# An LSTM step in two halves of its units: two gate banks, one product instruction, a state turned by halves

## The chip, the cores and the metric

The kernel runs on one core of a Trainium2 chip. The metric is the device time of one execution, in microseconds (us). Times shown are medians of several executions; the profile is of one more execution, and its own time stands beside its span, the time from its first to its last recorded instruction. PE is TensorE (PEld its weight loads), DVE is VectorE, ACT is ScalarE, POOL is GpSimd, SP is the engine that issues most DMAs.

## The reference

The input is x, 32 batches of 512 nodes by 256 features, in fp32, with an adjacency of integers. Two layers follow, each a graph attention and a feed-forward part, each on a layer norm of x and added to it:

```python
x = x + gnn0(layernorm(x), adj)      # typed attention, 4 heads
x = x + ffn0(layernorm(x))           # a Mamba-2 block
x = x + gnn1(layernorm(x), adj)      # one-head attention
x = x + ffn1(layernorm(x))           # an LSTM, with sums over its outputs
```

The last part is the one that matters here. It is an LSTM with 256 units over the 512 nodes as time:

```python
gates = xp + h @ W_hh.T                        # xp = x @ W_ih.T + b_ih + b_hh
i, f, g, o = split(gates, 4)
c = sigmoid(f) * c + sigmoid(i) * tanh(g)
h = sigmoid(o) * tanh(c)
```

Of its outputs, two logits for each step decide whether h enters a running sum; the result is 2 h plus the sum before the step times `fw_att` plus the sum after it times `bw_att`.

## The kernel before

Two phases follow each other. The first goes through the 32 batches one by one and does everything up to the LSTM (`layers_per_batch`); it leaves x in DRAM as X3, by time. It also reorders the LSTM's weights on POOL, between other work (`recurrence_weights`, with its helper `ordered`), into a DRAM tile. The second phase is `recurrence`: 512 steps for all 32 batches at once. There the program orders PE, DVE and ACT by hand: these engines run the instructions in the order of the code (`tc.manual_schedule`).

**Layout of a step.** The 256 units are four quarters (Q = 4) of 64 (J = 64). A quarter's results lie in 32 partitions (GB = 32, the batches), so that a [128, 64] tile holds all units of all batches. Sigmoids are computed as tanh of half the argument; the factors of one half are put into the weights, so that a step has tanh alone. `z` is a tile of 5 × 64 columns: the cell, then the four gates in the order forget, input, candidate, output.

**PE in a step.** `h_part` (L1260) adds the state's product with W_hh to the gates: for each part of the columns, each half k of the state (DK = 2) and each quarter q one matmul with 32 stationary columns, so that four of them stand side by side in the array. The parts are the forget gate (64 columns), input and candidate (128), output and the two logits (66), each in a PSUM bank of its own (tiles pg0, pg1, pg2). Then `x_part` (L1250) starts the next step's banks with its part of x: it turns the finished products of x (`xu`) through an identity. Then PE makes one eighth of the x products of a later group of 8 steps (`units`, L1236, two matmuls), and in 4 of 16 steps it first turns a normalised tile of x (L1174). A matmul of fp32 is two instructions in the profile.

**ACT and DVE in a step.** ACT takes one tanh for each part (L1320), later the tanh of the cell (L1330), then the copies out of PSUM (L1179, L1237). DVE makes two products in the tile `ab` (L1322 forget times cell, L1323 input times candidate), the new cell (L1328), the state hh (L1333) and its transpose by blocks of 32x32 into h (L1335), which is what PE's next h part waits for. Behind it come the masked state g (L1342, it reads the logits), the running sum pp (L1345), and one piece of extra work (`extra`: statistics and norms of later x, or a piece of the output of the 16 steps before, L1160 to L1213).

Buffers: z, ab, tc and h have three each (pool `st`); pg0 has one bank, pg1 and pg2 two each, pxt one and pu two, which fills the eight banks. In profile lines below, q and u of L630 are small tiles of the first phase.

Of the kernel before, what the change touches and what calls it, by code (L numbers as in the profile page):

```python
# [9 lines left out]
F32 = mybir.dt.float32  # L10
# [3 lines left out]
AF = mybir.ActivationFunctionType  # L14
ALU = mybir.AluOpType
# [4 lines left out]
P = 128  # L20
# [3 lines left out]
DK = D // P  # L24
# [9 lines left out]
GB = 32  # L34
# [995 lines left out]
def recurrence_weights(nc, pool, a, wr):  # L1030

    Q, J = 4, 64
    W = 4 * J + 2
    nx, nh = DK * Q * 4 * J, DK * Q * W
    n0 = nx + nh  # L1040
    half = (0.5, 0.5, 0.5, 1.0)
    for_x, for_h = (0, 3, 1, 2), (1, 0, 3, 2)

    def tile_(p, n, tag):
        return pool.tile([p, n], F32, tag=tag, name=tag)

    def ordered(raw, n, order, s):
        t = tile_(P, W, "rwt")
        nc.gpsimd.memset(t[:n, 4 * J :], 0.0)
        for to, g in enumerate(order):  # L1050
            nc.gpsimd.tensor_scalar(t[:n, to * J : (to + 1) * J], raw[:n, g * J : (g + 1) * J], half[g] * s, None, ALU.mult)
        return t


    wl = tile_(P, 2 * DK, "rwl")
    for q in range(Q):
        for l in range(2):
            nc.sync.dma_start(
                out=wl[q * 32 : (q + 1) * 32, l * DK : (l + 1) * DK],
                in_=a.wl[q : q + 1, l * J : (l + 1) * J].rearrange("o (k p) -> p (o k)", p=32),  # L1060
            )
    yield
    nc.gpsimd.tensor_tensor(wl[:, :DK], wl[:, DK:], wl[:, :DK], ALU.subtract)
    bl = tile_(P, 2, "rbl")
    nc.sync.dma_start(out=bl, in_=a.bl.to_broadcast([P, 2]))
    b = [tile_(P, 4 * J, f"rwraw{n}") for n in range(2)]
    for t, src in zip(b, (a.bih, a.bhh)):
        nc.sync.dma_start(out=t[:Q], in_=src.rearrange("o (q r) -> (o q) r", q=Q))
    yield
    nc.gpsimd.tensor_tensor(bl[:, 0:1], bl[:, 0:1], bl[:, 1:2], ALU.subtract)  # L1070
    nc.gpsimd.tensor_tensor(b[0][:Q], b[0][:Q], b[1][:Q], ALU.add)
    t = ordered(b[0], Q, for_x, 1.0)
    yield
    nc.sync.dma_start(out=wr[0][:, n0 + 2 * J + 8 : n0 + 2 * J + 9], in_=bl[:, 0:1])
    nc.sync.dma_start(out=wr[1].rearrange("o (q w) -> (o q) w", q=Q), in_=t[:Q, : 4 * J])
    yield
    nc.sync.dma_start(out=wr[0][:, n0 + 2 * J : n0 + 2 * J + 8], in_=wr[1].rearrange("o (u p) -> p (o u)", p=P))
    yield
    for n, src in enumerate((a.fw, a.bw)):
        t = tile_(P, W, "rwt")  # L1080
        for q in range(Q):
            nc.sync.dma_start(out=t[q * GB : (q + 1) * GB, :J], in_=src[q : q + 1, :].to_broadcast([GB, J]))
        yield
        nc.gpsimd.tensor_scalar(t[:, :J], t[:, :J], 0.5, None, ALU.mult)
        yield
        nc.sync.dma_start(out=wr[0][:, n0 + n * J : n0 + (n + 1) * J], in_=t[:, :J])
        yield
    for n, (src, s) in enumerate(((a.wih, 1.0), (a.whh, 0.5))):
        for k in range(DK):
            for q in range(Q):  # L1090
                raw = tile_(P, 4 * J, f"rwraw{q % 2}")
                cols = slice(q * 4 * J, (q + 1) * 4 * J)
                if n == 0:
                    nc.sync.dma_start(out=raw, in_=src[k * P : (k + 1) * P, cols])
                else:
                    for r in range(Q):
                        r0 = r * J + k * 32
                        nc.sync.dma_start(out=raw[r * 32 : (r + 1) * 32], in_=src[r0 : r0 + 32, cols])
                yield
                t = ordered(raw, P, (for_x, for_h)[n], s)  # L1100
                if n == 1:
                    nc.gpsimd.tensor_scalar(t[:, 4 * J : 4 * J + 1], wl[:, k : k + 1], 0.5, None, ALU.mult)
                yield
                w = (4 * J, W)[n]
                o0 = n * nx + (k * Q + q) * w
                nc.sync.dma_start(out=wr[0][:, o0 : o0 + w], in_=t[:, :w])
                yield


def recurrence(ctx, tc, c, a, X3, wr, out):  # L1110
# [3 lines left out]
    nc = tc.nc  # L1114
    T = X3.shape[0]
    Q, J = 4, 64
    W = 4 * J + 2
    G = CH // 2
    wp = ctx.enter_context(tc.tile_pool(name="rw", bufs=1))
    xp_ = ctx.enter_context(tc.tile_pool(name="rx", bufs=2))  # L1120
    st = ctx.enter_context(tc.tile_pool(name="rs", bufs=3))
# [115 lines left out]
        return lambda: nc.scalar.activation(xu[:, u, :], pu, AF.Identity, bias=bcol[:, u : u + 1])  # L1237


    PARTS = ((0, J), (J, 3 * J), (3 * J, W))  # L1240

    def x_part(t, xu):

        pg = [
            psg.tile([P, e - s], F32, tag=f"pg{n}", bufs=(1, 2, 2)[n], name=f"pg{n}_{t}") for n, (s, e) in enumerate(PARTS)
        ]
        r = (t % G) * GB
        for p, half, (s, e) in zip(pg, (1, 0, 1), ((0, J), (0, P), (J, P + 2))):
            for q in range(Q):
                nc.tensor.matmul(  # L1250
                    p[q * GB : (q + 1) * GB, :], xu[:, 2 * q + half, r : r + GB], turner[:, s:e],
                    start=True, stop=(t == 0),
                )
        return pg

    def h_part(pg, h, parts=PARTS, start=False):
        for p, (s, e) in zip(pg, parts):
            for k in range(DK):
                for q in range(Q):
                    nc.tensor.matmul(  # L1260
                        p[q * GB : (q + 1) * GB, :], h[:, k, :], whh[:, k, q, s:e],
                        start=(start and k == 0), stop=(k == DK - 1),
                    )

    with tc.manual_schedule(engines={mybir.EngineType.PE, mybir.EngineType.DVE, mybir.EngineType.Activation}):
        nxt = [None] * 2
# [7 lines left out]
        xu = {}  # L1274
# [2 lines left out]
        units(G, nxt[1], xu, 0)()  # L1277
        extra, turning = [], {}
        pg = x_part(0, xu[0])
        z = st.tile([P, 5 * J], F32, tag="z", name="z0")  # L1280
        nc.vector.memset(z[:, :J], 0.0)
        pp = ch.tile([P, CH + 1, J], F32, tag="pp", name="pp0")
        nc.vector.memset(pp[:, 0, :], 0.0)
        h = hh = None
        for t in range(T + 1):
# [14 lines left out]
                turning = {(5, 6, 10, 11)[n]: f for n, f in enumerate(turns)}  # L1300
            if last:

                pg = [psg.tile([P, W - 3 * J], F32, tag="pg2", name="pglast")]
                h_part(pg, h, PARTS[2:], True)
            elif t:
                h_part(pg, h)
            pgs = pg
            if not last:
                if t + 1 < T:
                    pg = x_part(t + 1, xu[(t + 1) // G * G])  # L1310

                g, u = divmod(t + 1, G)
                g = (g + 1) * G
                turned = [turning.pop(s)()] if s in turning else []
                if g < T:
                    turned.append(units(g, (xT if g < t0 + CH else nxt)[g // G % 2], xu, u))

                for (s0, e0), p in zip(PARTS, pgs):
                    e0 = min(e0, 4 * J)
                    nc.scalar.activation(z[:, J + s0 : J + e0], p[:, : e0 - s0], AF.Tanh)  # L1320
                ab = st.tile([P, 2 * J], F32, tag="ab", name=f"ab{t}")
                nc.vector.scalar_tensor_tensor(ab[:, :J], z[:, J : 2 * J], 1.0, z[:, :J], ALU.add, ALU.mult)  # L1322
                nc.vector.scalar_tensor_tensor(  # L1323
                    ab[:, J:], z[:, 2 * J : 3 * J], 1.0, z[:, 3 * J : 4 * J], ALU.add, ALU.mult
                )
                z2 = st.tile([P, 5 * J], F32, tag="z", name=f"z{t + 1}")
                cell = z2[:, :J]
                nc.vector.scalar_tensor_tensor(cell, ab[:, :J], 0.5, ab[:, J:], ALU.mult, ALU.add)  # L1328
                tc_ = st.tile([P, J], F32, tag="tc", name=f"tc{t}")
                nc.scalar.activation(tc_, cell, AF.Tanh, scale=0.5)  # L1330
                for f in turned:
                    f()
                nc.vector.scalar_tensor_tensor(hh[:, s, :], z[:, 4 * J :], 1.0, tc_, ALU.add, ALU.mult)  # L1333
                h = st.tile([P, DK, GB], F32, tag="h", name=f"h{t}")
                nc.vector.transpose(h.rearrange("p k b -> p (k b)"), hh[:, s, :])  # L1335
                z = z2
            if t:

                i = (t - 1) % CH
                p_, h_ = (pp_was, hh_was) if s == 0 and not last else (pp, hh)  # L1340
                g_ = st.tile([P, J], F32, tag="g", name=f"g{t}")
                nc.vector.scalar_tensor_tensor(  # L1342
                    g_, pgs[-1][:, J : J + 1].to_broadcast([P, J]), level, h_[:, i, :], ALU.is_gt, ALU.mult,
                )
                nc.vector.tensor_tensor(p_[:, i + 1, :], p_[:, i, :], g_, ALU.add)  # L1345
                if s == 0 and not last:
                    nc.vector.tensor_copy(pp[:, 0, :], p_[:, CH, :])
            if extra:
                extra.pop(0)()
        assert not extra and not turning  # L1350
        tot = wp.tile([P, J], F32, name="tot")
        nc.vector.tensor_tensor(tot, pp[:, CH, :], bw, ALU.mult)
# [112 lines left out]
```

## Time and profile before

| what | value |
|---|---|
| median of 3 executions | 4829.85 us (4828.24 to 4832.57) |
| the profiled execution, its time | 4838.21 us |
| its span | 4836.4 us |
| PE busy in the span | 4191.4 us (87%) |
| DVE busy | 3279.3 us (68%) |
| ACT busy | 3068.7 us (63%) |
| PE instructions | 52926 |
| granted TensorE clock, mean over the span | 0.965 |
| recurrence, first to last step | 3398 to 4768 us |

Busy PE is not PE at its peak, since matmuls overlap and their ends are modelled. A line of the timeline has a start in us from the span's start, a length, an engine, a line of the kernel, an operation, the tiles it writes and reads, the shapes and a count; several instructions in a row are merged into one line. A line of the groups has busy us and the mean ns of one, then the idle time ahead and what ended it. A line about one source line has the least, median and greatest duration in ns, and the first and last start in us. In the chain of waits, "issue" is time in which nothing that the profile shows was waited for, and ACTq is ACT's sequencer.

### The profile page before, as it was taken

How to read it: one execution, taken by the hardware profiler on the slowest of the kernel's cores; microseconds unless marked ns; L12 is line 12 of the kernel's file. 1: busy time of each engine (PE TensorE's matmuls, PEld its weight loads, DVE VectorE, ACT ScalarE, POOL GpSimd, SP SyncE). 2: the span in 40 equal slices, each digit the busy share in tenths (PEclk: the TensorE clock that was granted, in tenths of full speed). 3: DMA queues.
4: the chain of work that ended last, by engine and by line, in shares of the span. 5: the costliest groups of instructions: out<-in, count | busy, mean ns of one | idle time of the engine just before them, and what ended most of it. 6: DMA issues, size and time to landing. Idle time of an engine off the chain costs nothing. (4 is left out here: it accounts for less than half of the span.)

```text
span 4836.4 us, 126769 instructions
## 1 busy us (share of the span) xinstructions
PE 4191.4 (87%) x52926; PEld 2651.5 (55%) x52926; DVE 3279.3 (68%) x8670; ACT 3068.7 (63%) x6724; POOL 1308.8 (27%) x1012
## 2 busy tenths in 40 slices
PE   4888888888888888888888888886999999999993
PEld 2444444444554444544445444544777777777772
DVE  3567666676666666666666666664677777777776
ACT  2677667776677767677677776764555555555552
POOL 4333343333433334333343333431000000000000
PEclk7899999999999999999999999998999999999997
DMA  3221122211222112221112211111111111111115
GB/s 109 64 67 61 55 70 66 65 62 55 67 65 69 57 60 62 71 69 57 60 59 73 69 57 60 53 44 60 37 39 42 38 43 41 41 40 39 42 39 159
DMA packets 273746, 288.34 MB, mean 60 GB/s; under 512 B 152844, under 2 KB 224488, under 8 KB 270984
## 3 DMA queue, kind: packets, MB, share of 16 engines
q1 hardware_dynamic: 269784, 270.26, 19.0%
q10 hardware_dynamic: 3216, 9.81, 0.7%
q8 instruction: 418, 6.85, 0.6%
q14 instruction: 168, 1.38, 0.1%
q0 software_dynamic: 160, 0.04, 0.0%
HBM read 226.04 MB, written 37.11 MB: 54 GB/s over the span
## 5 line engine op out<-in xcount | busy, mean ns | idle before, releaser
L1260 PEld LDWEIGHTS pg<-wall,h 128*32 128x32 f32 x24528 | 476.7, 109 | 228.5 <-DVE h L1335 226.8
L1260 PE MATMUL pg<-wall,h 128*32 128x64 f32 x24528 | 561.2, 239 | 34.6 <-DVE h L1335 10.6
L1236 PE MATMUL pu<-xTr,wall 128*128 128x256 f32 x2048 | 565.5, 399 | 0.0
L467 DVE SCALAR_TENSOR_TENSOR w<-w,adjT 128x1024 f32<-128x1024 f32 x256 | 348.2, 1381 | 247.4 <-ACT w L461 247.4
L1320 ACT ACTIVATE z<-pg 128x64 f32<-128x64 f32 (+1 forms) x1536 | 345.8, 241 | 129.9 <-PE pg L1260 90.2
L1237 ACT ACTIVATE xu<-pu,wall 128x256 f32<-128x256 f32 x512 | 243.2, 475 | 278.6 <-PE pu L1236 278.6
L743 ACT ACTIVATE g<-bc,cs 128x128 f32<-128x128 f32 x1024 | 322.0, 391 | 139.7 <-PE py L811 139.7
L693 DVE SCALAR_TENSOR_TENSOR acc<-px,convw,acc 128x511 f32<-128x511 f32 (+2 forms) x480 | 347.3, 746 | 76.6 <-ACT acc L688 68.7
L461 ACT ACTIVATE w<-rb,neg,colsa 128x512 f32<-128x512 f32 x512 | 387.5, 806 | 10.2 <-DMA rb<-linea 5.8
L1236 PEld LDWEIGHTS pu<-xTr,wall 128*128 128x128 f32 x2048 | 348.8, 190 | 63.7
L533 PE MATMUL pav<-w,hb 128*64 128x512 f32 x1024 | 352.6, 615 | 21.9 <-DVE w L467 21.9
L830 PE MATMUL po<-wc,xh 128*128 128x256 f32 x1024 | 282.8, 422 | 96.8 <-POOL xh L800 96.8
L729 POOL TENSOR_TENSOR ce<-ce,cT 128x384 f32<-128x384 f32 x128 | 185.1, 1475 | 667.2 <-ACT cT L701 650.3
L54 POOL TENSOR_SCALAR ve<-mv 128x4 f32<-128x4 f32 x32 | 6.2, 193 | 1317.5 <-DVE mv L1161 1317.5
L1250 PE MATMUL pg<-turner,xu 128*32 128x64 f32 (+2 forms) x12288 | 324.3, 238 | 0.4 <-issue 0.3
L945 PE MATMUL pov<-wb,wv 128*128 128x257 f32 x1024 | 246.2, 393 | 90.4 <-DVE wv L467 90.4
L672 PE MATMUL px<-mT,win 128*128 128x512 f32 x640 | 306.9, 610 | 0.0
L830 PEld LDWEIGHTS po<-wc,xh 128*128 128x128 f32 x1024 | 203.1, 212 | 141.4 <-POOL xh L800 111.1
L1330 ACT ACTIVATE tc<-z 128x64 f32<-128x64 f32 x512 | 131.6, 257 | 224.1 <-DVE z L1328 224.1
L945 PEld LDWEIGHTS pov<-wb,wv 128*128 128x128 f32 x1024 | 193.6, 194 | 135.3 <-DVE wv L467 105.6
L1250 PEld LDWEIGHTS pg<-turner,xu 128*32 128x32 f32 x12288 | 265.6, 110 | 3.0 <-issue 1.8
L56 POOL TENSOR_TENSOR rs<-ve,mhalf 128x4 f32<-128x4 f32 (+1 forms) x192 | 256.0, 1334 | 15.9
(245 smaller groups left out, 8615.4 us busy)
## 6 DMA issues: line engine op xcount, KB each, us to landing
bc<-line SPq DMA_DIRECT2D x128, 512.0 KB
adj<-in_adj_dram SPq DMA_DIRECT2D x32, 1024.0 KB
rb<-linea SPq DMA_DIRECT2D x64, 512.0 KB
ce<-line SPq DMA_DIRECT2D x64, 384.0 KB
x<-in_x_dram SPq DMA_DIRECT2D x32, 512.0 KB
X<-x SPq DMA_DIRECT2D x32, 512.0 KB
xt<-X SPq DMA_DIRECT2D x128, 128.0 KB
x<-X SPq DMA_DIRECT2D x128, 128.0 KB
```

Of the source, the lines that this page charges most:

```text
L461: nc.scalar.activation(w[:, t, k, :], rb[:, k, :], AF.Relu, bias=neg1, scale=cols[:, 2 * m + t, h + k : h + k + 1],)
L467: nc.vector.scalar_tensor_tensor(w[:, :, k, :], w[:, :, k, :], 1.0, edges, ALU.add, ALU.mult)
L533: nc.tensor.matmul(pa[k * HO : (k + 1) * HO, :], hb[:, j, 2 * q + k, :], w[:, t, k, :], start=(j == 0), stop=(j == NT - 1),)
L672: nc.tensor.matmul(pz, win[:, k, col : col + P], mT[:, k, :], start=(k == 0), stop=(k == DK - 1))
L693: nc.vector.scalar_tensor_tensor(acc[:, s:], pz[:, : N - s], convw[:, cc, k : k + 1], acc[:, s:], ALU.mult, ALU.add)
L743: nc.scalar.activation(g[:, i, k, :], bc[:, k, i * P : (i + 1) * P], AF.Relu, bias=cs[:, i, 2 * cc + k : 2 * cc + k + 1], scale=-1.0,)
L830: nc.tensor.matmul(po[:, i * D : (i + 1) * D], xh[:, cc, it * P : (it + 1) * P], wc[:, cc, :], start=(cc == 0), stop=(cc == NC - 1),)
L945: nc.tensor.matmul(po[:, : D + 1], ws[j // 2][:, j % 2, 0, it * P : (it + 1) * P], wb[:, j, :], start=(j == 0), stop=(j == NT - 1),)
L1236: nc.tensor.matmul(pu, wih[:, k, u, :], xT[:, k, :], start=(k == 0), stop=(k == DK - 1))
L1250: nc.tensor.matmul(p[q * GB : (q + 1) * GB, :], xu[:, 2 * q + half, r : r + GB], turner[:, s:e], start=True, stop=(t == 0),)
L1260: nc.tensor.matmul(p[q * GB : (q + 1) * GB, :], h[:, k, :], whh[:, k, q, s:e], start=(start and k == 0), stop=(k == DK - 1),)
L1320: nc.scalar.activation(z[:, J + s0 : J + e0], p[:, : e0 - s0], AF.Tanh)
```

## The change

Each quarter's 64 units are cut into two halves of 32 (H = 32). The weights are reordered so that the columns of a quarter are: all four gates of the first half, then all four of the second, then the logits. The gates' order becomes candidate, forget, input, output (`order = (3, 1, 0, 2)`; the launch puts them as input 0, forget 1, output 2, candidate 3). With the cell ahead of them in z, [cell, candidate] and [forget, input] are two blocks of equal width.

There are now two banks a step, one for each half, with 128 and 130 columns, two buffers each. The h part goes k by k: both banks for k = 0, then both for k = 1. ACT takes one tanh of 128 columns for each half. One DVE instruction makes both products of a half. The cell, its tanh, the state and its transpose are made for each half, and h is two tiles; k = 0 needs the first alone. The extra piece moves from behind pp to between g and pp.

```diff
@@ -1034,21 +1034,24 @@
...
     half = (0.5, 0.5, 0.5, 1.0)
-    for_x, for_h = (0, 3, 1, 2), (1, 0, 3, 2)
+    order = (3, 1, 0, 2)
     def tile_(p, n, tag):
         return pool.tile([p, n], F32, tag=tag, name=tag)
-    def ordered(raw, n, order, s):
+    def ordered(raw, n, s):
         t = tile_(P, W, "rwt")
         nc.gpsimd.memset(t[:n, 4 * J :], 0.0)
+        halves = t[:n, : 4 * J].rearrange("p (e g j) -> p e g j", e=2, g=4)
         for to, g in enumerate(order):
-            nc.gpsimd.tensor_scalar(t[:n, to * J : (to + 1) * J], raw[:n, g * J : (g + 1) * J], half[g] * s, None, ALU.mult)
+            src = raw[:n, g * J : (g + 1) * J].rearrange("p (e j) -> p e j", e=2)
+            nc.gpsimd.tensor_scalar(halves[:, :, to, :], src, half[g] * s, None, ALU.mult)
         return t
@@ -1069,7 +1072,7 @@
     yield
     nc.gpsimd.tensor_tensor(bl[:, 0:1], bl[:, 0:1], bl[:, 1:2], ALU.subtract)
     nc.gpsimd.tensor_tensor(b[0][:Q], b[0][:Q], b[1][:Q], ALU.add)
-    t = ordered(b[0], Q, for_x, 1.0)
+    t = ordered(b[0], Q, 1.0)
     yield
     nc.sync.dma_start(out=wr[0][:, n0 + 2 * J + 8 : n0 + 2 * J + 9], in_=bl[:, 0:1])
     nc.sync.dma_start(out=wr[1].rearrange("o (q w) -> (o q) w", q=Q), in_=t[:Q, : 4 * J])
@@ -1097,7 +1100,7 @@
                         r0 = r * J + k * 32
                         nc.sync.dma_start(out=raw[r * 32 : (r + 1) * 32], in_=src[r0 : r0 + 32, cols])
                 yield
-                t = ordered(raw, P, (for_x, for_h)[n], s)
+                t = ordered(raw, P, s)
                 if n == 1:
                     nc.gpsimd.tensor_scalar(t[:, 4 * J : 4 * J + 1], wl[:, k : k + 1], 0.5, None, ALU.mult)
                 yield
@@ -1114,6 +1117,7 @@
     nc = tc.nc
     T = X3.shape[0]
     Q, J = 4, 64
+    H = J // 2
     W = 4 * J + 2
     G = CH // 2
     wp = ctx.enter_context(tc.tile_pool(name="rw", bufs=1))
@@ -1237,30 +1241,28 @@
         return lambda: nc.scalar.activation(xu[:, u, :], pu, AF.Identity, bias=bcol[:, u : u + 1])
-    PARTS = ((0, J), (J, 3 * J), (3 * J, W))
+    PARTS = ((0, 4 * H), (4 * H, W))
     def x_part(t, xu):
-        pg = [
-            psg.tile([P, e - s], F32, tag=f"pg{n}", bufs=(1, 2, 2)[n], name=f"pg{n}_{t}") for n, (s, e) in enumerate(PARTS)
-        ]
+        pg = [psg.tile([P, e - s], F32, tag=f"pg{n}", name=f"pg{n}_{t}") for n, (s, e) in enumerate(PARTS)]
         r = (t % G) * GB
-        for p, half, (s, e) in zip(pg, (1, 0, 1), ((0, J), (0, P), (J, P + 2))):
+        for n, (p, (s, e)) in enumerate(zip(pg, PARTS)):
             for q in range(Q):
                 nc.tensor.matmul(
-                    p[q * GB : (q + 1) * GB, :], xu[:, 2 * q + half, r : r + GB], turner[:, s:e],
+                    p[q * GB : (q + 1) * GB, :], xu[:, 2 * q + n, r : r + GB], turner[:, : e - s],
                     start=True, stop=(t == 0),
                 )
         return pg
-    def h_part(pg, h, parts=PARTS, start=False):
-        for p, (s, e) in zip(pg, parts):
-            for k in range(DK):
-                for q in range(Q):
-                    nc.tensor.matmul(
-                        p[q * GB : (q + 1) * GB, :], h[:, k, :], whh[:, k, q, s:e],
-                        start=(start and k == 0), stop=(k == DK - 1),
-                    )
+    def h_part(pg, h, order, start=False):
+        for k, n in order:
+            p, (s, e) = pg[n], PARTS[n]
+            for q in range(Q):
+                nc.tensor.matmul(
+                    p[q * GB : (q + 1) * GB, :], h[k], whh[:, k, q, s:e], start=(start and k == 0), stop=(k == DK - 1)
+                )
     with tc.manual_schedule(engines={mybir.EngineType.PE, mybir.EngineType.DVE, mybir.EngineType.Activation}):
         nxt = [None] * 2
@@ -1277,8 +1279,10 @@
         units(G, nxt[1], xu, 0)()
         extra, turning = [], {}
         pg = x_part(0, xu[0])
-        z = st.tile([P, 5 * J], F32, tag="z", name="z0")
-        nc.vector.memset(z[:, :J], 0.0)
+        z = [st.tile([P, 5 * H], F32, tag=f"z{n}", name=f"z{n}_0") for n in range(2)]
+        for n in range(2):
+            nc.vector.memset(z[n][:, :H], 0.0)
         pp = ch.tile([P, CH + 1, J], F32, tag="pp", name="pp0")
         nc.vector.memset(pp[:, 0, :], 0.0)
         h = hh = None
@@ -1300,10 +1304,10 @@
                 turning = {(5, 6, 10, 11)[n]: f for n, f in enumerate(turns)}
             if last:
-                pg = [psg.tile([P, W - 3 * J], F32, tag="pg2", name="pglast")]
-                h_part(pg, h, PARTS[2:], True)
+                pg = [None, psg.tile([P, W - 4 * H], F32, tag="pg1", name="pglast")]
+                h_part(pg, h, ((0, 1), (1, 1)), True)
             elif t:
-                h_part(pg, h)
+                h_part(pg, h, ((0, 0), (0, 1), (1, 0), (1, 1)))
             pgs = pg
             if not last:
                 if t + 1 < T:
@@ -1315,38 +1319,41 @@
                 if g < T:
                     turned.append(units(g, (xT if g < t0 + CH else nxt)[g // G % 2], xu, u))
-                for (s0, e0), p in zip(PARTS, pgs):
-                    e0 = min(e0, 4 * J)
-                    nc.scalar.activation(z[:, J + s0 : J + e0], p[:, : e0 - s0], AF.Tanh)
-                ab = st.tile([P, 2 * J], F32, tag="ab", name=f"ab{t}")
-                nc.vector.scalar_tensor_tensor(ab[:, :J], z[:, J : 2 * J], 1.0, z[:, :J], ALU.add, ALU.mult)
-                nc.vector.scalar_tensor_tensor(
-                    ab[:, J:], z[:, 2 * J : 3 * J], 1.0, z[:, 3 * J : 4 * J], ALU.add, ALU.mult
-                )
-                z2 = st.tile([P, 5 * J], F32, tag="z", name=f"z{t + 1}")
-                cell = z2[:, :J]
-                nc.vector.scalar_tensor_tensor(cell, ab[:, :J], 0.5, ab[:, J:], ALU.mult, ALU.add)
-                tc_ = st.tile([P, J], F32, tag="tc", name=f"tc{t}")
-                nc.scalar.activation(tc_, cell, AF.Tanh, scale=0.5)
+                for n in range(2):
+                    nc.scalar.activation(z[n][:, H:], pgs[n][:, : 4 * H], AF.Tanh)
+                z2 = [st.tile([P, 5 * H], F32, tag=f"z{n}", name=f"z{n}_{t + 1}") for n in range(2)]
+                for n in range(2):
+                    ab = st.tile([P, 2 * H], F32, tag=f"ab{n}", name=f"ab{n}_{t}")
+                    nc.vector.scalar_tensor_tensor(ab, z[n][:, 2 * H : 4 * H], 1.0, z[n][:, : 2 * H], ALU.add, ALU.mult)
+                    nc.vector.scalar_tensor_tensor(z2[n][:, :H], ab[:, :H], 0.5, ab[:, H:], ALU.mult, ALU.add)
+                tcs = []
+                for n in range(2):
+                    tcs.append(st.tile([P, H], F32, tag=f"tc{n}", name=f"tc{n}_{t}"))
+                    nc.scalar.activation(tcs[n], z2[n][:, :H], AF.Tanh, scale=0.5)
                 for f in turned:
                     f()
-                nc.vector.scalar_tensor_tensor(hh[:, s, :], z[:, 4 * J :], 1.0, tc_, ALU.add, ALU.mult)
-                h = st.tile([P, DK, GB], F32, tag="h", name=f"h{t}")
-                nc.vector.transpose(h.rearrange("p k b -> p (k b)"), hh[:, s, :])
+                h = []
+                for n in range(2):
+                    part = hh[:, s, n * H : (n + 1) * H]
+                    nc.vector.scalar_tensor_tensor(part, z[n][:, 4 * H :], 1.0, tcs[n], ALU.add, ALU.mult)
+                    h.append(st.tile([P, GB], F32, tag=f"h{n}", name=f"h{n}_{t}"))
+                    nc.vector.transpose(h[n], part)
                 z = z2
             if t:
                 i = (t - 1) % CH
                 p_, h_ = (pp_was, hh_was) if s == 0 and not last else (pp, hh)
                 g_ = st.tile([P, J], F32, tag="g", name=f"g{t}")
+                l0 = 4 * H
                 nc.vector.scalar_tensor_tensor(
-                    g_, pgs[-1][:, J : J + 1].to_broadcast([P, J]), level, h_[:, i, :], ALU.is_gt, ALU.mult,
-                )
+                    g_, pgs[-1][:, l0 : l0 + 1].to_broadcast([P, J]), level, h_[:, i, :], ALU.is_gt, ALU.mult,
+                )
+            if extra and not last:
+                extra.pop(0)()
+            if t:
                 nc.vector.tensor_tensor(p_[:, i + 1, :], p_[:, i, :], g_, ALU.add)
                 if s == 0 and not last:
                     nc.vector.tensor_copy(pp[:, 0, :], p_[:, CH, :])
-            if extra:
-                extra.pop(0)()
         assert not extra and not turning
         tot = wp.tile([P, J], F32, name="tot")
         nc.vector.tensor_tensor(tot, pp[:, CH, :], bw, ALU.mult)
```

## The prediction

> **What bounds the kernel now.** I read the slices of the span first: from about 3398 us on PE stands at 9 tenths, POOL at nothing, and the pattern doesn't change until the end. That is the recurrence, the only part whose executed order the change touches. Its transposes (L1335) begin at 3398.2 and the 511th at 4767.5, so 511 steps take (4767.5 − 3398.2)/510 = 2.685 us each, 1372 us of a span of 4836.4. Next I asked for the chain of waits of one plain step, in which each piece has its start, its length and its engine:
>
> ```profile
> 4019.02 0.91 PE pg L1260 x32
> ...
> 4019.96 0.29 ACT z L1320
> ...
> 4020.27 0.24 DVE ab L1323
> ...
> 4020.53 0.24 DVE z L1328
> 4020.76 0.02 issue
> 4020.78 0.02 ACTq L1330
> 4020.80 0.04 issue
> 4020.84 0.27 ACT tc L1330
> ...
> 4021.14 0.24 DVE hh L1333
> ...
> 4021.39 0.26 DVE h L1335
> 4021.65 0.04 issue
> 4021.69 0.31 PE pg L1260 x6
> ```
>
> Start to start: PE to tanh 0.94, to product 0.31, to cell 0.26, to the cell's tanh 0.31, to hh 0.30, to the transpose 0.25, to the next PE 0.30: 2.67 us. A step is one closed ring through three engines, and no engine is full in it. Note the cell's tanh: other hand-overs show 0.02 of issue, this one shows ACT's sequencer (ACTq) and another 0.04 between. Asking for line 1320 and line 1330 shows why:
>
> ```profile
> L1320 ACTq EVENT_SEMAPHORE  x509: 17/17/17, 3404.3 to 4768.3; - x170
> L1330 ACTq EVENT_SEMAPHORE  x509: 17/17/17, 3405.6 to 4769.6; - x170
> ```
>
> 509 = 512 − 3: from the fourth step on, the first tanh into a z buffer and the tanh into a tc buffer (three buffers each) wait on two semaphores, and the second wait takes an extra instruction. In the trace it puts the ACTIVATE 62 ns later. In the kernel before, one of these is on the ring (tc). The other belongs to the forget gate's tanh, which is early; the 128-wide tanh on the ring waits once.
>
> How near PE is as the next bound, from the timeline of PE in a plain step and one that also turns x:
>
> ```profile
> 4019.94 0.63 PE L1250 MATMUL pg<-turner,xu 128*32 128x64 f32 x24
> 4020.49 1.13 PE L1236 MATMUL pu<-xTr,wall 128*128 128x256 f32 x4
> 4021.69 0.32 PE L1260 MATMUL pg<-wall,h 128*32 128x64 f32 x8
> ...
> 4024.37 1.10 PE L1260 MATMUL pg<-wall,h 128*32 128x64 f32 x48
> ...
> 4026.12 1.03 PE L1236 MATMUL pu<-xTr,wall 128*128 128x256 f32 x4
> 4027.07 1.10 PE L1260 MATMUL pg<-wall,h 128*32 128x64 f32 x48
> ```
>
> The turning step takes 2.70 (the next, to 4029.78, 2.71), with PE back to back: 4026.12 to 4027.07 is 0.95 for the four unit matmuls, already loaded. In a plain step they start at 4020.49, after 1.47 of h and x parts, and with 0.11 for the first weights would be over at 1.47 + 0.11 + 0.95 = 2.53. So PE has 0.14 us of slack in 12 of 16 steps, and none in the 4 that turn x.
>
> Prices used:
>
> ```profile
> L1260 PE MATMUL pg<-wall,h 128*32 128x128 f32 x8176 | 317.3, 272 | 0.0
> L1320 ACT ACTIVATE z<-pg 128x128 f32<-128x128 f32 x511 | 141.8, 278 | 78.1 <-PE pg L1260 78.1
> L1330 ACT ACTIVATE tc<-z 128x64 f32<-128x64 f32 x511 | 131.3, 257 | 223.7 <-DVE z L1328 223.7
> L1335 DVE STREAM_TRANSPOSE h<-hh 128x64 f32<-128x64 f32 x511 | 125.3, 245 | 17.6
> L630 DVE SCALAR_TENSOR_TENSOR q<-q,u x32: 191/192/193, 126.3 to 3266.0; 128x32 f32<-128x32 f32 x32
> ```
>
> **What the Trainium skill says.** "VectorE: DVE Perf Modes", section on the TRN2 errata, gives an fp32 two-input operation (N + 151)/0.96 ns: 224 for 64 elements, 191 for 32. The trace agrees (225 and the 192 of L630), so halving a shape saves 33 ns, not half. "ScalarE: Activation LUTs", What ACT_TABLE_LOAD costs, has 0.833 ns an element and an overlap of 93 ns between ACTIVATEs in a row; here 128 against 64 wide from PSUM is 278 − 223 = 55, or 0.86 an element, so 32 fewer save 27. "TensorEngine Tiling (Array Packing)", Key Properties, says that changing the tiling mode drains TensorE; the trace shows some 0.09 us between the 32-column and the 128-column matmuls, both ways, which no merging here removes. "TensorE: Matmul & The Clock Gate", Part 3, The mechanism, says that matmuls keep program order; the trace's starts agree. So a second half that isn't ready holds all behind it. No page bears on the two-semaphore wait.
>
> **The change part by part, from one step.** *Matmuls.* The h part has the same columns: (64 + 128 + 66) for each k and quarter before, (128 + 130) after. The ring's tanh waited for 4 × (64 + 128) = 768 columns before; now z0 waits for both banks of k = 0 and the first of k = 1, 2 × (128 + 130 + 128) = 772 (a matmul is two instructions). So PE to tanh stays 0.94. Merging saves a little: the trace starts quartets of 64-wide instructions 0.056 apart and 128-wide ones 0.109, so a merged pair saves 0.003, and six of them 0.02 a step. It matters only where PE binds: the turning step 2.706 becomes 2.69, the plain PE bound 2.51.
>
> *First tanh.* Its shape is 128x128 as before (278 ns), but it is now the first toucher of its own three-deep buffer, so it inherits the two-semaphore wait: +0.06, to 1.00. Both ends: 0 if one wait suffices; no more than the 0.062 of tc otherwise. I take 0.06, since z keeps three buffers and its order of first users.
>
> *Products.* One instruction makes both, with 64 elements out: start to cell 0.26 as L1323 has it. The separate forget product (L1322) goes; it was done early and off the ring.
>
> *Cell, tanh, hh, transpose by halves:* −33, −27, −33 ns from the prices above. The 32-wide transpose isn't in the trace: at best −33 like other VectorE work, at worst 0; I take −33. The steps are 0.28, 0.27, 0.22, 0.27. The tanh at worst stays 257.
>
> Sum of the ring: 1.00 + 0.31 + 0.26 + 0.28 + 0.27 + 0.22 + 0.27 = 2.61 against 2.67; unrounded +62 − 33 − 27 − 33 − 33 = −64 ns.
>
> *The second half* must hide. With 0 where PE ends z0's last matmul: z1's bank ends at 0.222, its tanh starts at 0.348 and ends at 0.626. VectorE meanwhile: ab0 0.436, cell0 0.697, ab1 from about 0.81 (spacing of independent 32-wide work, an estimate: 0.11, between the 0.109 after the 64-wide copy and the 0.143 after L1345), cell1 1.07; tc0 runs 0.983 to 1.213, hh0 starts at 1.245, 0.06 after VectorE is free of cell1. Then T0 1.472, hh1 about 1.61, T1 1.84 to 2.05, PE 2.10. PE starts k = 0 at 1.737 and has 0.44 of it, till about 2.18, so T1 is hidden by 0.08. Without that cover each ns of lateness goes on the ring.
>
> *Moved order.* g, then the extra, then pp instead of g, pp, extra. g reads the logits, long there; the extra fills pp's wait for g. After T1 at 1.84: g 1.97, extra 2.12, at most 0.64 (two norms, 0.322 apart each), pp 2.76, free 2.90; the next ab0 is due at 2.61 + 0.436 = 3.04. It costs nothing, at 0.14 from the edge; behind it stands only ab0. The extra's DMA issues stay on SP, behind the same instructions. ACT's xu ends some 0.5 after the next h part starts, before z0 is due at 1.00; before, it was as early and its tanh was due sooner. The weights' reordering on POOL has as many instructions as before, outside the recurrence: 0.
>
> *All steps:* 12 of 16 save 0.064, 4 (PE-bound) 0.018: 0.0525 a step, × 511 = 27 us. The profiled execution took 4838.2 for a span of 4836.4; its span becomes 4810. The median shown is 8.4 below that execution; I subtract from it: 4829.85 − 27 = 4803.
>
> **Rivals.** *No second wait at z0.* For it: other tanhs of L1320 have one wait. Against: the 509 events. Then plain steps take 2.545, still over PE's 2.51, and save 0.126: (12 × 0.126 + 4 × 0.018)/16 × 511 = 51 us, 4779. If more fell away, PE would stop it at 2.51: 64 us, 4766.
>
> *Small shapes don't shrink.* If the 32-wide transpose and tanh cost what the 64-wide do, 60 ns return and plain steps save 4 ns: 4 us in all, 4826. Against it stand 0.86 ns an element on ACT and L630 on VectorE; the transpose is open.
>
> *Slower: VectorE's order holds hh0.* In its queue ab1 and cell1 stand ahead of hh0. With spacing s after a 32-wide instruction, hh0 can't start before 0.958 + 2s. Up to s = 0.14 this is hidden behind tc0; at s = 0.18 the whole gain is gone; with no overlap at all (s = 0.226) hh0 starts at 1.41, a step takes 2.77 and the kernel 47 us more: 4877. For it: a waiting instruction blocks this queue, and the margin is 0.06. Against: independent VectorE instructions overlap in every view here, 0.143 after 225 ns and 0.109 after 195.
>
> **How the numbers follow.** Forecast 0.54, one wait 0.20, no shrinking 0.09, held VectorE 0.17. The time is the forecast's, 4803 (its own range 4792 to 4814). The range 4766 to 4840 runs from PE's floor to past the no-shrink case, and leaves out the slower one. 0.2% is 9.7 us, about what a measurement of this kernel can tell from no change. Faster: 0.54 + 0.20 and a little of the third, 0.76; same 0.07; slower 0.17.
>
> **What will show it.** PE instructions fall by 24 a step, to about 40,650. Plain steps 2.61 and turning steps 2.69. EVENT_SEMAPHORE 1018 times on the gates' tanh line, 1018 on the cell's. VectorE 32-wide 192, transpose 212, tanh 230. hh0 waits for ACT, and k = 1's matmuls never for T1. Wrong if hh0 starts on VectorE's order instead of tc0, if PE idles between the k halves, or if ab0 starts late behind pp.

## The result, and the profile after

The changed kernel takes 4802.18 us (median of 4 executions, 4798.48 to 4803.97) against 4829.05 for the kernel before on the same chip: a ratio of 0.9944, with a 95% interval of 0.9931 to 0.9956, or 27 us. The forecast was 4803, faster.

The profiled execution took 4803.97 us with a span of 4802.2. Between the two profiled spans lie 34.2 us. Of these 28.1 are the recurrence (511 steps of 2.630 instead of 2.685 us, from the starts of the transposes in the trace); the other 6 are the first phase, which ended at 3391.6 instead of 3398.2. They are not put down to the change: that phase ends anywhere from 3383.6 to 3394.1 in the nine profiles of the experiments below, and the medians, 26.9 us apart, leave no room for it beside the recurrence.

A plain step is one of the 12 in 16 without a turn of x, a turning step one of the other 4. The tiles and instructions of the first half carry a 0 in the text (z0, tc0, hh0), those of the second a 1. The timeline of a plain step of the changed kernel (start, length, engine, line, operation):

```profile
4002.08 1.09 PE L1263 MATMUL pg<-wall,h 128*32 128x128 f32 x32
...
4003.08 0.50 ACT L1323 ACTIVATE z<-pg 128x128 f32<-128x128 f32 x2 [0.48 <-PE pg L1263]
4003.39 0.23 DVE L1327 SCALAR_TENSOR_TENSOR ab<-z 128x64 f32<-128x64 f32 x1
...
4003.65 0.19 DVE L1328 SCALAR_TENSOR_TENSOR z<-ab 128x32 f32<-128x32 f32 x1
4003.76 0.21 DVE L1327 SCALAR_TENSOR_TENSOR ab<-z 128x64 f32<-128x64 f32 x1
4003.93 0.59 ACT L1332 ACTIVATE tc<-z 128x32 f32<-128x32 f32 x2 [0.36 <-DVE z L1328]
4004.01 0.19 DVE L1328 SCALAR_TENSOR_TENSOR z<-ab 128x32 f32<-128x32 f32 x1
4004.19 0.19 DVE L1338 SCALAR_TENSOR_TENSOR hh<-z,tc 128x32 f32<-128x32 f32 x1
4004.42 0.21 DVE L1340 STREAM_TRANSPOSE h<-hh 128x32 f32<-128x32 f32 x1
4004.55 0.19 DVE L1338 SCALAR_TENSOR_TENSOR hh<-z,tc 128x32 f32<-128x32 f32 x1
...
4004.69 1.09 PE L1263 MATMUL pg<-wall,h 128*32 128x128 f32 x32
```

Read it as the forecast's sum: PE to tanh 1.00, to product 0.31, to cell 0.26, to the cell's tanh 0.28, to hh 0.26, to the transpose 0.23, to PE 0.27: 2.61, as forecast. Over all plain steps the median is 2.60. The second half's instructions stand between those of the first, in gaps that were idle.

The same views of the changed kernel as were shown of before: the two lines' waits on two semaphores, PE's timeline through two steps that turn x, and the shapes that got smaller.

```profile
L1323 ACTq EVENT_SEMAPHORE  x1018: 17/17/17, 3397.9 to 4734.4; - x170
L1332 ACTq EVENT_SEMAPHORE  x1018: 17/17/17, 3398.8 to 4735.4; - x170
```

```profile
4035.24 1.03 PE L1240 MATMUL pu<-xTr,wall 128*128 128x256 f32 x4
4036.20 1.09 PE L1263 MATMUL pg<-wall,h 128*32 128x128 f32 x32
...
4037.94 1.03 PE L1240 MATMUL pu<-xTr,wall 128*128 128x256 f32 x4
4038.90 1.09 PE L1263 MATMUL pg<-wall,h 128*32 128x128 f32 x32
```

```profile
L1332 ACT ACTIVATE tc<-z 128x32 f32<-128x32 f32 x1024 | 234.4, 229 | 250.6 <-DVE z L1328 181.7 <-DVE hh L1338 2.5
L1340 DVE STREAM_TRANSPOSE h<-hh 128x32 f32<-128x32 f32 x1024 | 216.7, 212 | 34.8
L1328 DVE SCALAR_TENSOR_TENSOR z<-ab 128x32 f32<-128x32 f32 x1024 | 196.3, 192 | 35.0
```

All four tanhs of a step now wait on two semaphores (1018 = 2 × 509 for each line). A turning step takes 2.70 and is bound by PE as before. The small shapes cost 229, 212 and 192 ns.

One view of the changed kernel contradicts all this at first sight. Its chain of waits goes through PE alone:

```profile
4014.21 1.06 PE pu L1240 x4
4015.27 0.01 issue
4015.28 1.09 PE pg L1263 x31
4016.37 0.44 PE pg L1252 x14
4016.81 1.06 PE pu L1240 x4
4017.87 0.01 issue
4017.88 1.09 PE pg L1263 x30
```

Taken at its word, PE is now the bound of every step. But the ends of matmuls are modelled, and a listed end doesn't say when the next matmul could start: in the turning steps above the unit matmuls are listed until 4038.97 (4037.94 + 1.03), and the h part starts at 4038.90. In plain steps the last unit matmul's listed end falls, by chance, where the next h part begins. Starts are the better guide. Where PE runs back to back, in the turning steps, the h part starts 0.309 after the start of the last unit matmul; in the plain steps of the changed kernel it starts 0.386 after (medians of the trace), so PE stands idle for 0.08. And in the timeline above the first transpose ends at 4004.63 (4004.42 + 0.21) and PE starts 0.05 after, the same distance as in the kernel before. So there were two readings of the result, ring or PE; the starts speak for the ring, and the first two experiments test it.

### The profile page after: what moved, and what is told of

It is laid out like the page before. It is cut to its first block, busy times and chain, and to the rows that moved or that the text cites. A ratio compares the mean times of both kernels' runs of the same rounds, so it can differ in the third digit from the quotient of the medians.

```text
span 4802.2 us, 105289 instructions
## 1 busy us (share of the span) xinstructions
PE 4177.1 (87%) x40654; PEld 2586.4 (54%) x40654; DVE 3438.4 (72%) x10207; ACT 3084.4 (64%) x6724; POOL 1308.3 (27%) x1012
## 5 line engine op out<-in xcount | busy, mean ns | idle before, releaser
L1263 PE MATMUL pg<-wall,h 128*32 128x128 f32 x16352 | 559.1, 276 | 13.6 <-DVE h L1340 10.3
L1263 PEld LDWEIGHTS pg<-wall,h 128*32 128x32 f32 x16352 | 419.2, 109 | 210.1 <-DVE h L1340 170.1
L1323 ACT ACTIVATE z<-pg 128x128 f32<-128x128 f32 x1024 | 255.8, 278 | 249.6 <-PE pg L1263 248.6
L1332 ACT ACTIVATE tc<-z 128x32 f32<-128x32 f32 x1024 | 234.4, 229 | 250.6 <-DVE z L1328 181.7
L1252 PE MATMUL pg<-turner,xu 128*32 128x128 f32 (+1 forms) x8192 | 321.5, 273 | 0.0
L1327 DVE SCALAR_TENSOR_TENSOR ab<-z 128x64 f32<-128x64 f32 x1024 | 226.4, 221 | 83.0 <-ACT z L1323 57.0
```

What stands on the lines that cost most here:

```text
L1252: nc.tensor.matmul(p[q * GB : (q + 1) * GB, :], xu[:, 2 * q + n, r : r + GB], turner[:, : e - s], start=True, stop=(t == 0),)
L1263: nc.tensor.matmul(p[q * GB : (q + 1) * GB, :], h[k], whh[:, k, q, s:e], start=(start and k == 0), stop=(k == DK - 1))
L1323: nc.scalar.activation(z[n][:, H:], pgs[n][:, : 4 * H], AF.Tanh)
```

## The experiments

Steps below are medians of the distance between transposes of the first half over the 12 plain and the 4 turning steps of 16. The changed kernel has 2.60 and 2.70. Ratios are to the kernel before, timed on the same chip.

**Four buffers for each z tile.** In the two lines that make z:

```diff
-        z = [st.tile([P, 5 * H], F32, tag=f"z{n}", name=f"z{n}_0") for n in range(2)]
+        z = [st.tile([P, 5 * H], F32, tag=f"z{n}", bufs=4, name=f"z{n}_0") for n in range(2)]
```

> The changed kernel, with four buffers instead of three for each z tile. Theory (a ring through three engines): the first ACT user of a z buffer no longer has to wait for ACT's own work three steps back, so the extra wait instruction ahead of both gate tanhs goes, and the ring's share of it, 0.06 us, with it: plain steps 2.60 to 2.54, turning steps 2.70 as now, about 4779 us. Rival (the chain of waits of the changed kernel, in which PE follows PE through the whole recurrence, so PE is the bound): plain steps stay 2.60, about 4802 us.

Measured: 4775.13 us, ratio 0.9883 (0.9867 to 0.9898); plain steps 2.54, turning 2.70. No extra wait is left on L1323, the 1018 on L1332 stay. The two steps in PE's timeline:

```profile
4008.03 1.09 PE L1263 MATMUL pg<-wall,h 128*32 128x128 f32 x32
4010.58 1.09 PE L1263 MATMUL pg<-wall,h 128*32 128x128 f32 x32
```

Nothing was taken from PE, and the step shrank by 0.06: PE did not bind the changed kernel's plain steps, and the extra wait was worth what the forecast put it at. The recurrence is 51 us shorter than before (1321.1 instead of 1372.0), as the rival with one wait had it. The chain of waits of this run shows PE alone again, so that view can't settle the question here.

**One wait on two semaphores a step.**

```diff
-                z2 = [st.tile([P, 5 * H], F32, tag=f"z{n}", name=f"z{n}_{t + 1}") for n in range(2)]
+                z2 = [st.tile([P, 5 * H], F32, tag=f"z{n}", bufs=(4, 3)[n], name=f"z{n}_{t + 1}") for n in range(2)]
-                    tcs.append(st.tile([P, H], F32, tag=f"tc{n}", name=f"tc{n}_{t}"))
+                    tcs.append(st.tile([P, H], F32, tag=f"tc{n}", bufs=4, name=f"tc{n}_{t}"))
```

> The changed kernel with four buffers for z of the first half and for both tc tiles, three for z of the second half, so that only the second half's gate tanh waits on two semaphores. Theory: the ring loses 0.12 us and would take 2.48, so that PE binds plain steps at 2.51 to 2.52; turning steps 2.70; about 4769 us. Rival that PE binds already: no change, 4802 us.

Measured: 4767.59 us, ratio 0.9869 (0.9854 to 0.9884); plain 2.52, turning 2.70; 509 extra waits in all. Its timeline:

```profile
4008.58 0.21 DVE L1340 STREAM_TRANSPOSE h<-hh 128x32 f32<-128x32 f32 x1
4008.89 1.09 PE L1263 MATMUL pg<-wall,h 128*32 128x128 f32 x32
...
4011.41 0.86 PE L1263 MATMUL pg<-wall,h 128*32 128x128 f32 x23
```

Here the transpose ends at 4008.79 and PE starts 0.10 after, not 0.05: now PE is late, by 0.04, and the step stopped at PE's floor, 2.52 where 2.51 had been worked out, instead of the ring's 2.48. The h part now starts 0.309 after the last unit matmul in plain steps too, as where PE runs back to back. That makes this version the fastest: 63 us below the kernel before, more than twice the change's gain.

**The kernel before with four tc buffers.**

```diff
-                tc_ = st.tile([P, J], F32, tag="tc", name=f"tc{t}")
+                tc_ = st.tile([P, J], F32, tag="tc", bufs=4, name=f"tc{t}")
```

> The kernel before, with four buffers instead of three for tc. Theory: the extra wait ahead of the cell's tanh goes, 0.06 us of the ring; plain steps 2.67 to 2.61, turning steps 2.71 as before, since PE binds them: about 24 us less, 4805 us, which is what the whole change brings. Rival (the extra wait instruction lies in time that another wait covers): no change, 4829 us.

Measured: 4811.93 us, ratio 0.9960 (0.9947 to 0.9974); plain 2.61, turning 2.71, and no extra wait is left on L1330. The steps are those expected. The total is 19 us less rather than 24; the recurrence itself is 22 us shorter (511 × (2.685 − 2.642)). One number in the code brings some 70% of what the whole change does in the medians (19 of 27 us), and 22 of 28 us in the recurrence.

**The extra piece behind pp again** (in the changed kernel):

```diff
-            if extra and not last:
-                extra.pop(0)()
-            if t:
                 nc.vector.tensor_tensor(p_[:, i + 1, :], p_[:, i, :], g_, ALU.add)
                 if s == 0 and not last:
                     nc.vector.tensor_copy(pp[:, 0, :], p_[:, CH, :])
+            if extra and not last:
+                extra.pop(0)()
```

> The changed kernel with the extra piece put back behind pp. Theory: VectorE has 0.13 us of slack a step and loses it to pp's wait for g, so plain steps stay 2.60; only the first of 16 steps, which has a copy and a statistic too, grows by some 0.1: 0 to 6 us more, 4802 to 4808 us. Rival (the moved piece is part of the gain): some 0.05 us or more in each step with an extra, 20 us and more.

Measured: 4807.77 us, ratio 0.9956 (0.9942 to 0.9970). Plain steps stay 2.60; only the first of 16 rises, to 2.70. 0.095 × 32 such steps are 3 us. The moved piece is no part of the gain worth naming; its worth is in one step of 16.

**One or two idle products ahead of hh0**, of operands that lie ready:

```diff
+                nc.vector.scalar_tensor_tensor(st.tile([P, H], F32, tag="idle0", ...), bw[:, :H], 1.0, fw[:, :H], ALU.add, ALU.mult)
                 h = []
                 for n in range(2):
```

> The changed kernel with one unneeded 32-wide VectorE product a step, between the second half's cell and the first half's state. Theory: it takes 0.11 us of VectorE's order, of which 0.07 is hidden behind the tanh of the first cell; plain steps 2.60 to 2.64, turning steps as now: about 15 us more, 4817 us. Rival (PE is the bound): no change.

> The same with two such products. Theory: 0.22 less the same 0.07: plain steps 2.75, turning steps 2.75: some 65 us more, 4867 us. The difference to the run with one is the spacing of one VectorE instruction, 0.11 us; what is missing of the first is the slack.

Measured: with one 4805.34 us, ratio 0.9957 (0.9941 to 0.9974), plain 2.621; with two 4848.03 us, ratio 1.0045 (1.0028 to 1.0062), plain and turning 2.725. The first product costs 0.020, the second 0.104. So one 32-wide instruction takes 0.104 of VectorE's order, and 0.084 of it was free (0.06 in the forecast, 0.07 in the expectation). Both steps come out some 0.02 below what was expected (2.64 and 2.75), and both totals with them (4817 and 4867), because the free share was put too low and, with two, each instruction slightly too high. The timeline with two:

```profile
4007.48 0.59 ACT L1332 ACTIVATE tc<-z 128x32 f32<-128x32 f32 x2 [0.36 <-DVE z L1328]
4007.55 0.19 DVE L1328 SCALAR_TENSOR_TENSOR z<-ab 128x32 f32<-128x32 f32 x1
4007.66 0.18 DVE L1335 SCALAR_TENSOR_TENSOR idle<-wall 128x32 f32<-128x32 f32 x1
4007.76 0.18 DVE L1336 SCALAR_TENSOR_TENSOR idle<-wall 128x32 f32<-128x32 f32 x1
4007.87 0.18 DVE L1340 SCALAR_TENSOR_TENSOR hh<-z,tc 128x32 f32<-128x32 f32 x1
```

hh0 starts 0.11 after the last idle product, while its tanh was over at 4007.71 (4007.48 + 0.23): the slower rival's mechanism is real, and it sets in with the first added instruction. Two instructions turn the gain into a loss.

**Two idle products ahead of hh1 alone** (the same lines, inside the loop, `if n:`).

> The changed kernel with two unneeded 32-wide VectorE products ahead of the second half's state, so that the second transpose comes 0.22 us later and the first one when it does now. Theory: 0.08 to 0.10 us of it is hidden behind the four quartets of k = 0; the rest, 0.12 to 0.14, is on the ring: plain steps about 2.73, turning steps about 2.74, 50 us more. If the second half had no need to be hidden: no change.

Measured: 4831.77 us, ratio 1.0017 (1.0011 to 1.0024); plain 2.69, turning 2.70. The expectation of 2.73 was too high, and the timeline shows the term:

```profile
4007.95 0.21 DVE L1343 STREAM_TRANSPOSE h<-hh 128x32 f32<-128x32 f32 x1
4008.09 0.15 DVE L1339 SCALAR_TENSOR_TENSOR idle<-wall 128x32 f32<-128x32 f32 x1
4008.15 0.19 DVE L1340 SCALAR_TENSOR_TENSOR idle<-wall 128x32 f32<-128x32 f32 x1
...
4008.22 1.17 PE L1263 MATMUL pg<-wall,h 128*32 128x128 f32 x32
...
4008.47 0.21 DVE L1343 STREAM_TRANSPOSE h<-hh 128x32 f32<-128x32 f32 x1
```

The second product started only 0.06 after the first, so the second transpose came 0.52 after the first instead of 0.36: 0.16 late, not 0.22. In the trace the matmuls of k = 1 then start 0.06 late, so the cover was 0.10, where the forecast had 0.08; and the first four of them hold the next four up by another 0.02. That makes the 0.09 that reached the step, and the h part is listed with 1.17 instead of 1.09. So the second half is hidden, but barely.

**The state in one piece**, the banks, gate tanhs and products by halves as in the change. z becomes one tile with a halves dimension, and:

```diff
-                    nc.vector.scalar_tensor_tensor(z2[n][:, :H], ab[:, :H], 0.5, ab[:, H:], ALU.mult, ALU.add)
+                nc.vector.scalar_tensor_tensor(z2[:, :, :H], ab[:, :, :H], 0.5, ab[:, :, H:], ALU.mult, ALU.add)
```

and so for the cell's tanh, hh and the transpose.

> The changed kernel with its two banks, two gate tanhs and product instructions, but the cell, its tanh, the state and the transpose done once for all 64 units. Theory: the ring then runs through the second bank: 1.09 to the end of both banks, 0.06 to the tanh, and the old 64-wide durations: 2.89 us in every step, some 135 us more than the changed kernel, 4937 us. If two banks alone brought the gain: no more than the changed kernel.

Measured: 4934.2 us, ratio 1.0229 (1.0212 to 1.0246); every step 2.90.

```profile
4007.95 1.09 PE L1263 MATMUL pg<-wall,h 128*32 128x128 f32 x32 [0.30 <-DVE h L1337]
...
4010.00 0.26 ACT L1330 ACTIVATE tc<-z 128x64 f32<-128x64 f32 x1 [0.61 <-DVE z L1328]
...
4010.85 1.09 PE L1263 MATMUL pg<-wall,h 128*32 128x128 f32 x32 [0.30 <-DVE h L1337]
```

Two banks of all gates alone lose: the ring then runs through both, while before it had left the output gate's bank aside. From PE's start to the tanh on the ring it is 1.17 (the median in the trace) instead of 0.93 before, and the other pieces of the ring are as they were. Only with the state in halves do the banks pay. No run took the order of the h part, k by k, away alone.

**The two products in two instructions** (in the changed kernel):

```diff
-                    nc.vector.scalar_tensor_tensor(ab, z[n][:, 2 * H : 4 * H], 1.0, z[n][:, : 2 * H], ALU.add, ALU.mult)
+                    for m in range(2):
+                        nc.vector.scalar_tensor_tensor(
+                            ab[:, m * H : (m + 1) * H], z[n][:, (2 + m) * H : (3 + m) * H], 1.0, z[n][:, m * H : (m + 1) * H],
+                            ALU.add, ALU.mult,
+                        )
```

> The changed kernel with the two products of each half in two 32-wide VectorE instructions instead of one of 64. Theory: the first half's second product starts some 0.10 later, the first cell waits for it (0.10 + 0.19 + 0.03 instead of 0.26), 0.07 on the ring; four instructions then stand between the first cell and hh0 on VectorE, which adds 0.01 to 0.02: plain steps 2.60 to 2.68, turning steps 2.70 as now: about 31 us more than the changed kernel, 4833 us. If the product instruction were hidden: no change.

Measured: 4831.29 us, ratio 1.0001 (0.9992 to 1.0009); plain 2.67, turning 2.70.

```profile
4009.90 0.29 DVE L1328 SCALAR_TENSOR_TENSOR ab<-z 128x32 f32<-128x32 f32 x2
4010.23 0.19 DVE L1332 SCALAR_TENSOR_TENSOR z<-ab 128x32 f32<-128x32 f32 x1
```

Product to cell is 0.33 instead of 0.26, and the whole gain is gone. The 0.01 to 0.02 that was expected on top, from one more instruction ahead of hh0, did not show. The merged product doesn't bring the gain by itself, since the kernel before had but one product on its ring; without it the halves, as built here with three buffers for z, bring nothing.

## Why the prediction was right, point by point

- **Ring and its first tanh.** Forecast 2.61 with the inherited wait, measured 2.60. The experiment with four z buffers puts that wait at 0.06, by taking it away. The rival with one wait at z0 fell in the changed kernel and came true, step for step, once the buffers were there: 2.545 forecast, 2.54 measured. Start to start, each piece of the ring changed by what was forecast to within 3 ns (+59, −34, −28, −33, −35 ns where +62, −33, −27, −33, −33 had been put).
- **Small shapes.** −33, −27, −33, −33 ns were forecast; 257 to 229, 225 to 192 (cell) and 191 (hh), and 245 to 212 were measured. The transpose, the only price that stood open, shrank like the rest; the no-shrink rival fell. The overlap of ACTIVATEs in a row, which the forecast names but doesn't use in its sum, is 0.10 where it can be seen, in the run with the state in one piece.
- **Turning steps.** Forecast 2.69, measured 2.70, in all runs of the changed kernel but those whose ring is longer. The PE floor of plain steps, 2.51, was shown as 2.52 in the run with one double wait. In both, the merging of the matmuls saved about half of the 0.018 of the forecast: a turning step went from 2.706 to 2.698, and the x part starts 0.904 after the h part instead of 0.914.
- **PE's instructions.** 40,654 against about 40,650.
- **The second half's cover.** 0.08 forecast, 0.10 measured by making it late; a late second half costs 0.02 more than its lateness.
- **VectorE's order.** The margin of 0.06 was 0.084 by the steps with idle products. The profile shows hardly any waits of hh for the tanh (1.9 us in all), contrary to what "hh0 waits for ACT" would make one look for: VectorE is still busy with the second cell until hh0 starts. That hh0 starts for the tanh is seen in the 0.03 from the tanh's end (4003.93 + 0.23) to 4004.19, and in the free 0.084.
- **The moved extra.** Forecast at nothing; put back, it cost 3 us in one step of 16.
- **The sum.** 0.0525 a step was forecast and 0.055 measured; the difference is 1 us. It is that small by some luck: the plain steps saved 0.071 instead of 0.064, the turning steps 0.008 instead of 0.018, and the two partly cancel.

## What to carry to other kernels

When a loop is a ring through several engines, price a change by its start-to-start distances and count each wait on the ring, the buffers' included: here a fourth buffer for three small tiles took another 33 us off the recurrence, where the rewritten step had taken 28. In these runs the halves paid only as long as nothing of the second half, or added between the two, delayed the first, so work out the cover of the second half and the order of the shared engine before building it. Where a chain of waits names an engine whose ends are modelled, check it against starts (the engine's own where it runs back to back, and its start after the other engine's end), or take a piece off the ring and see whether the step shrinks.

## What the runs showed of the hardware

In these kernels an ACTIVATE that waited on its own engine's earlier work besides another engine's had a second instruction ahead of it in ACT's queue, and it started some 0.06 us later: without it a step went from 2.671 to 2.612 in the kernel before and from 2.600 to 2.542 in the changed one. With one more buffer in the rotation it is gone (509 to none on the cell's tanh before, 1018 to none on the gates' tanh after); the runs don't show why the fourth buffer is enough. PE's queue got such an instruction too, ahead of the x part (L1252, 509 in the changed kernel, none before), and there it cost nothing visible: the x part starts 0.11 after the last four matmuls of the h part, the distance within the h part.

Independent 32-wide VectorE instructions followed each other at 0.10 us here, for lengths of 0.18 to 0.19, and, in the run with a late second half, two behind a transpose at 0.06. When the second half of the state came late, the first matmul of k = 1 took 297 ns instead of 273 in the trace, as the first of the h part does in every step of the changed kernel, and the next four started 0.133 after it instead of 0.110.
